# Order of the matmul pieces in the attention loop of a two-layer convolutional attention kernel: two scores side by side, later mixing

## The chip, the core and the metric

The kernel runs on one core of one Trainium2 chip. A core has five engines that run beside each other and wait for one another by semaphores: PE (TensorE, matrix products, with a weight load of its own that the profile calls PEld), DVE (VectorE), ACT (ScalarE), POOL (GpSimd) and SP (SyncE, which here only issues DMAs). The metric is the device time of one execution, in microseconds (us); lower is better.

## The reference, cut to what matters

Two attention layers run one after the other on x (8 images, 512 channels, 32 x 32 = 1024 tokens). The change touches the second layer alone. With 8 heads of 64 channels it computes, for every image b:

```python
q, k, v = (einsum('oc,bct->bot', w, xf).reshape(b, heads, hd, t) for w in (w_q, w_k, w_v))
attn = einsum('bhdq,bhdT->bhqT', q, k) * scale
attn = einsum('gh,bhqT->bgqT', w_head, attn)      # mixes the eight heads
attn = softmax(attn, axis=-1)
attn = (attn - mean) / sqrt(var + EPS)            # over all of a head's q and T
attn = attn * in_gamma + in_beta
out  = einsum('bhqT,bhdT->bhqd', attn, v)         # then w_proj, bias, residual
```

Each softmax needs the mixed scores of all heads, so the scores have to be regrouped between the two products: the first product gives one head at a time, the second wants the eight heads of a query beside each other on the partitions.

## The kernel before, in words

Everything here is in the class Attention1 (line 1616) and the loop over images at line 1901. For an image the 1024 queries are cut into NT = 8 blocks p of 128 queries. The work on a block has five stations:

- **scores(p, i)**, lines 1624 to 1643, i = 0 to 7: PE multiplies q and k for two heads and half of the keys (i = 0 to 3 are the first half, kh = 0; i = 4 to 7 the second, kh = 1) into a PSUM tile "m" of two banks. ACT copies it into an SBUF tile "raw" (L1643); for p = 0, DVE copies the odd ones (L1641). There are two raw buffers, so kh = 0 always has the one and kh = 1 the other.
- **regroup(kh, s)**, lines 1645 to 1650: SP issues two DMAs of 256 KB that read raw with a stride of partitions and write the tile "re", of which there is one. The four s are four sets of queries. A pair (kh, s) can start when the four copies of its half are done, and when the mixing of the block before has read its part of re.
- **mix(p, s)**, lines 1658 to 1682: PE multiplies re with the mixing weights into two PSUM tiles "m", each of which ACT turns into exponentials (L1676) in the tile "e" (two buffers). The call returns a function that issues the second of the two exponentials, so a caller can put other work between.
- **flip and moments**, lines 1684 to 1704: DVE transposes e into "et" (L1691) and takes statistics of e (L1702, four instructions). Once a block is complete, sums(p) (L1744 to L1748) turns them into "zz", and totals(p) (PE, L1755) multiplies zz; the reciprocals follow on DVE.
- **values(p, u, parts)**, lines 1706 to 1724: PE multiplies et and v (L1718) into the PSUM tile "a"; u is a half of the query sets, and the four parts of a half are a quarter each. leave(p, u), lines 1726 to 1737, copies the result out on ACT (L1734).

The PSUM tiles "m" come from a pool with three buffers (line 1273). Scores and mixings take them in turn, in the order in which they are called, so a piece waits until the tile three calls back has been copied or exponentiated. The engines take their instructions strictly in the order in which the program lists them.

**step(p, t, ag)**, line 1845, writes out that order by hand. For each p it is called with t = 0 to 3, and it works on three blocks at a time: the scores of block p, the mixing, flip and moments of block p - 1, and the rest of the values of block p - 2. For 2 <= p <= 7 PE's order is, with S for a score, M for a mixing, V for a part of the values, VV for two parts and z for the totals:

- t = 0: S0 S1 S2, VV (half 0 of block p - 2), M0
- t = 1: V (half 1, part 0), z, S3, M1
- t = 2: S4, V (half 1, part 1), S5, M2, VV (half 1, parts 2 and 3)
- t = 3: S6, M3, V (half 0 of block p - 1, part 0), S7, V (part 1)

M3's second exponentials are issued after S7's copy. DMAs go to SP's queue at the end of t = 1 (regroup of (0,0) and (0,1)), t = 2 ((0,2)) and t = 3 ((0,3), (1,0), (1,1), (1,2), (1,3)). At the end of t = 0, four or five further loads for the next image are queued there ("pieces", 128 KB each, L1304 and L1339). The agenda `ag` adds other work at fixed slots; its half-number slots hold entries only for p = 8.

In every image p = 0 has scores alone, p = 1 has no values of a block p - 2, and p = 8 has no scores; there, products for the next image (L1383) stand between the mixings.

Of the kernel before, what the change touches and what calls it, by code (L numbers as in the profile page):

```python
# [467 lines left out]
def tile_two_attention_layers(  # L468
# [19 lines left out]
    nc = tc.nc  # L488
# [205 lines left out]
    with ExitStack() as l0:  # L694
# [505 lines left out]
        for b in range(B):  # L1200
            more = b + 1 < B
            ag = Agenda()
# [61 lines left out]
    with ExitStack() as l1:  # L1264
# [180 lines left out]
        def k_leave():  # L1445
            for fn in due:
                fn()
            due.clear()
# [167 lines left out]
        class Attention1:  # L1616
# [228 lines left out]
            def step(self, p, t, ag):  # L1845

                new, old, older = p < NT, p >= 1, p >= 2
                if new and t != 1:
                    self.scores(p, 2 * t)
                    if t == 0:  # L1850
                        self.scores(p, 1)
                        self.scores(p, 2)
                if t == 3 and old:
                    second = self.mix(p - 1, 3)
                if t == 0 and older:
                    self.values(p - 2, 0, 2, 3)
                    self.leave(p - 2, 0)
                    self.sums(p - 2)
                    if p % 2 == 0 and p >= 4:
                        self.divide(p // 2 - 2, nc.gpsimd)  # L1860
                if t in (1, 2) and older:
                    self.values(p - 2, 1, t - 1)
                    if t == 1:
                        self.flip(p - 1, 0)
                        self.totals(p - 2)
                        self.moments(p - 1, 0)
                if t == 3 and old:
                    self.values(p - 1, 0, 0)
                if new and t:
                    self.scores(p, 2 * t + 1)  # L1870
                if t == 3 and old:
                    second()
                    self.values(p - 1, 0, 1)
                if t < 3 and old:
                    self.mix(p - 1, t)()
                ag.run(4 * p + t - 0.5)
                if t == 2 and older:
                    self.values(p - 2, 1, 2, 3)
                    self.leave(p - 2, 1)
                k_leave()  # L1880
                if p == 1 or old and t:
                    self.flip(p - 1, t)
                    self.moments(p - 1, t)
                if new:
                    for kh, s in (
                        (), ((0, 0), (0, 1)), ((0, 2),), ((0, 3), (1, 0), (1, 1), (1, 2), (1, 3)),
                    )[t]:
                        self.regroup(kh, s)
                if old and t == 0:
                    self.piece(4 if p < 5 else 5)  # L1890
                ag.run(4 * p + t)
# [9 lines left out]
        for b in range(B):  # L1901
            more = b + 1 < B
            a = Attention1(b)
            ag = Agenda()
# [142 lines left out]
```

## Time and profile before

| quantity | value |
|---|---|
| time, median of 3 runs (lowest, highest) | 4043.96 us (4040.07, 4045.96) |
| time of the profiled execution | 4037.07 us |
| its span, from the first to the last instruction | 4035.0 us |
| mean granted TensorE clock | 0.994 |
| PE busy | 3929.8 us (97%) |
| DVE busy | 2836.2 us (70%) |
| ACT busy | 1976.2 us (49%) |
| POOL busy | 129.1 us (3%) |
| regroup DMAs (re<-raw) | 1024 issues of 256 KB |
| scores of the second layer (L1631) | 523.8 us busy |
| mixings (L1665) | 352.8 us busy, idle before them 36.8 us |
| values (L1718) | 556.2 us busy |
| exponentials (L1676) | 502.9 us busy, 1023 ns each |
| copies into raw (L1643) | 471.3 us busy, 1017 ns each |
| flips (L1691) | 587.3 us busy, 2294 ns each |
| moments (L1702) | 633.8 us busy, 674 ns each |

The page gives each engine's busy time and its share of the span. A busy PE is not a PE without stalls: ends of matmuls are modelled, and a matmul that is held up in the middle of a group of sixteen counts as busy. What a piece costs is therefore read from the timeline, as the distance from its first matmul to the first matmul of the next piece. The second layer begins at about 1800 us of the span. One "round" below is the stretch from one z of the timeline to the next.

### The profile page before, as it was taken

The numbers are of one execution on the slowest core, as the hardware profiler recorded it, in microseconds if no ns is written. First come the engines' busy times: TensorE is split into PE (matmuls) and PEld (weight loads), VectorE is DVE, ScalarE is ACT, GpSimd is POOL, SyncE is SP. The second block draws the span as 40 slices with busy tenths as digits, with TensorE's granted clock in tenths as the row PEclk, the third lists the DMA queues.
The fourth block names the chain that finished last, engine by engine and source line by source line (L and its number), as shares of the span: only waits on it lengthen the run. The fifth ranks groups of instructions, "written<-read, shape, count | busy, mean of one in ns | idle before, by whom it ended". The sixth has DMA issues, their size and how long they took to land. (4 is left out here: it accounts for less than half of the span.)

```text
span 4035.0 us, 95990 instructions
## 1 busy us (share of the span) xinstructions
PE 3929.8 (97%) x41932; PEld 1825.9 (45%) x41932; DVE 2836.2 (70%) x4124; ACT 1976.2 (49%) x2431; POOL 129.1 (3%) x150
## 2 busy tenths in 40 slices
PE   8999999999999999999999999999999999999997
PEld 4353535343443435344544544544544444445354
DVE  4748475756667575847949859769769679588597
ACT  1727263544535362616617437347257166175274
POOL 0000000000000000000000001000000000000010
PEclk9999999999999999999999999999999999999998
DMA  3313131211111211227738739559469287396384
GB/s 126 113 47 116 45 119 48 87 41 58 72 66 51 82 56 61 77 80 201 195 116 222 194 105 233 157 144 232 131 168 226 93 213 201 106 224 187 112 216 127
DMA packets 268636, 519.12 MB, mean 129 GB/s; under 512 B 49840, under 2 KB 84912, under 8 KB 261552
## 3 DMA queue, kind: packets, MB, share of 16 engines
q1 hardware_dynamic: 261664, 497.96, 43.1%
q0 software_dynamic: 6544, 14.94, 1.5%
q8 instruction: 331, 5.42, 0.6%
q14 instruction: 97, 0.79, 0.1%
HBM read 197.16 MB, written 46.92 MB: 60 GB/s over the span
## 5 line engine op out<-in xcount | busy, mean ns | idle before, releaser
L1691 DVE STREAM_TRANSPOSE et<-e 128x2048 f32<-128x2048 f32 x256 | 587.3, 2294 | 115.7 <-ACT e L1676 110.2
L1718 PEld LDWEIGHTS a<-et,v 128*64 128x64 f32 x16384 | 508.4, 138 | 287.7 <-issue 228.3
L1702 DVE BATCH_NORM_STATS2 bn<-e 128x6 f32<-128x512 f32 x1024 | 633.8, 674 | 0.0
L1086 ACT ACTIVATE e<-s 128x1024 f32<-128x1024 f32 x512 | 497.2, 1026 | 234.5 <-PE s L1081 234.0
L1643 ACT COPY raw<-s 128x1024 f32<-128x1024 f32 x480 | 471.3, 1017 | 276.6 <-PE s L1631 243.7
L1676 ACT ACTIVATE e<-m 128x1024 f32<-128x1024 f32 x512 | 502.9, 1023 | 148.6 <-PE m L1665 63.1
L1718 PE MATMUL a<-et,v 128*64 128x64 f32 x16384 | 556.2, 225 | 5.7 <-DVE et L1691 5.3
L1094 DVE TENSOR_TENSOR zacc<-zacc,e 128x1024 f32<-128x1024 f32 x384 | 468.7, 1221 | 89.9 <-ACT e L1086 68.0
L1631 PE MATMUL s<-k,q 64*64 64x512 f32 x4096 | 523.8, 608 | 8.0 <-DVE q L1497 3.1
L1081 PE MATMUL s<-q,k 64*64 64x512 f32 x4096 | 490.1, 593 | 2.3 <-ACT e L1086 2.3
L1107 PE MATMUL a<-e,v 64*64 64x512 f32 x4096 | 484.1, 589 | 0.0
L1665 PE MATMUL m<-re,wmix 32*32 32x512 f32 x8192 | 352.8, 606 | 36.8 <-DMA re<-raw 30.7
L1107 PEld LDWEIGHTS a<-e,v 64*64 64x64 f32 x4096 | 156.7, 133 | 282.8 <-issue 282.5
L1081 PEld LDWEIGHTS s<-q,k 64*64 64x64 f32 x4096 | 147.9, 133 | 275.2 <-issue 241.0
L1458 PE MATMUL pv<-wv,y 128*128 128x512 f32 x480 | 213.8, 601 | 0.0
L1631 PEld LDWEIGHTS s<-k,q 64*64 64x64 f32 x4096 | 121.7, 131 | 201.6 <-issue 81.4
L1665 PEld LDWEIGHTS m<-re,wmix 32*32 32x32 f32 x8192 | 73.4, 103 | 232.9 <-ACT e L1676 68.0
L1734 ACT COPY q<-a 64x256 f32<-64x256 f32 x256 | 93.8, 366 | 139.8 <-PE a L1718 137.4
L1770 POOL DMA_DIRECT2D zd<-rz x56 | 34.6, 619 | 3466.4 <-DMA y<-x 1854.0
L1458 PEld LDWEIGHTS pv<-wv,y 128*128 128x128 f32 x480 | 89.9, 191 | 118.0 <-issue 111.3
L1462 ACT COPY v<-pv 128x512 f32<-128x512 f32 x30 | 17.6, 585 | 220.4 <-PE pv L1458 220.4
L1092 DVE TENSOR_TENSOR zacc<-e,e 128x1024 f32<-128x1024 f32 x64 | 78.3, 1223 | 56.1 <-ACT e L1086 56.1
(315 smaller groups left out, 3946.8 us busy)
## 6 DMA issues: line engine op xcount, KB each, us to landing
re<-raw SPq DMA_DIRECT2D x1024, 256.0 KB
left_q<-left_q SPq DMA_DIRECT2D x17, 1792.0 KB
left_p<-left_p SPq DMA_DIRECT2D x17, 1792.0 KB
left_k<-left_k SPq DMA_DIRECT2D x10, 1792.0 KB
x<-in_x_dram SPq DMA_DIRECT2D x32, 512.0 KB
rzb<-zd SPq DMA_DIRECT2D x128, 128.0 KB
x<-x SPq DMA_DIRECT2D x64, 256.0 KB
left_v<-left_v SPq DMA_DIRECT2D x8, 1792.0 KB
```

The costliest lines, as they stand in the source:

```text
L1081: nc.tensor.matmul(ps[c * D : c * D + D, m], k[r, hp, k0 : k0 + D], q[r, hp, ts(f, FB)], start=True, stop=True,)
L1086: nc.scalar.activation(e[i], ps, AF.Exp, scale=S0 * S0)
L1094: nc.vector.tensor_add(zacc[g], zacc[g], e[i])
L1107: nc.tensor.matmul(acc[g][a][m * D : m * D + D], v[rows, kc, ts(2 * hp + m, D)], e[i][rows, m], start=(kc == 0), stop=(kc == NG - 1),)
L1458: nc.tensor.matmul(ps[:, m], y_t[b][:, c, ts(2 * i + m, P)], w[:, c], start=(c == 0), stop=(c == NCC - 1),)
L1631: nc.tensor.matmul(ps[c * D : c * D + D, m], qo_t[b][r, p, hp, ts(c, D)], k_t[b][r, hp, ts(kh, FB)], start=True, stop=True,)
L1643: nc.scalar.copy(dst, ps)
L1665: nc.tensor.matmul(ps[a // 2][c * 32 : c * 32 + 32, a % 2].rearrange("p (r kb k) -> p r kb k", r=2, k=32), wmix[rows].rearrange("p g i -> ...
L1676: nc.scalar.activation(e[:, :, 2 * h : 2 * h + 2].rearrange("p r a k -> p a r k"), ps[h].rearrange("p a (r k) -> p a r k", r=2), AF.Exp,)
L1691: nc.vector.transpose(self.et[p, u].rearrange("p kb (r st a) g q -> p st kb r (a g q)", r=2, st=2)[:, st], self.e[p, s].rearrange("p r a ( ...
L1702: nc.vector.bn_stats(self.bn[p][:, s, a], e[:, :, a].rearrange("p r k -> p k r"))
L1718: nc.tensor.matmul(acc[two * D : two * D + D, s].rearrange("p (x q) -> p x q", q=4), v_t[b][:, kb, ts(g, D)], et[:, kb, :, g], start=(kb = ...
```

## The change

Only the body of step changes; the same pieces are issued, and each the same number of times. For t = 0 and t = 1 the order stays. For 2 <= p <= 7 the order of t = 2 and t = 3 on PE becomes:

- t = 2: V (half 1, part 1), S4, S5, VV (half 1, parts 2 and 3), M2
- t = 3: S6, V (half 0, part 0), M3, S7, V (part 1)

On ACT, leave(p - 2, 1) now stands ahead of M2's exponentials; S4's and S5's copies stay ahead of both. M3's first exponentials still stand ahead of S7's copy and the second ones behind it. DVE's order and SP's order stay as they are: flip 2, moments 2 and the regroup of (0,2) are listed after M2 in both. For p = 1, which has no values of a block p - 2, only t = 3 changes. For p = 0 and p = 8 nothing changes.

```diff
@@ -1845,38 +1845,58 @@
             def step(self, p, t, ag):
 
                 new, old, older = p < NT, p >= 1, p >= 2
-                if new and t != 1:
-                    self.scores(p, 2 * t)
-                    if t == 0:
-                        self.scores(p, 1)
-                        self.scores(p, 2)
-                if t == 3 and old:
-                    second = self.mix(p - 1, 3)
-                if t == 0 and older:
-                    self.values(p - 2, 0, 2, 3)
-                    self.leave(p - 2, 0)
-                    self.sums(p - 2)
-                    if p % 2 == 0 and p >= 4:
-                        self.divide(p // 2 - 2, nc.gpsimd)
-                if t in (1, 2) and older:
-                    self.values(p - 2, 1, t - 1)
-                    if t == 1:
+                if t == 0:
+                    if new:
+                        for i in range(3):
+                            self.scores(p, i)
+                    if older:
+                        self.values(p - 2, 0, 2, 3)
+                        self.leave(p - 2, 0)
+                        self.sums(p - 2)
+                        if p % 2 == 0 and p >= 4:
+                            self.divide(p // 2 - 2, nc.gpsimd)
+                    if old:
+                        self.mix(p - 1, 0)()
+                    ag.run(4 * p - 0.5)
+                elif t == 1:
+                    if older:
+                        self.values(p - 2, 1, 0)
                         self.flip(p - 1, 0)
                         self.totals(p - 2)
                         self.moments(p - 1, 0)
-                if t == 3 and old:
-                    self.values(p - 1, 0, 0)
-                if new and t:
-                    self.scores(p, 2 * t + 1)
-                if t == 3 and old:
-                    second()
-                    self.values(p - 1, 0, 1)
-                if t < 3 and old:
-                    self.mix(p - 1, t)()
-                ag.run(4 * p + t - 0.5)
-                if t == 2 and older:
-                    self.values(p - 2, 1, 2, 3)
-                    self.leave(p - 2, 1)
+                    if new:
+                        self.scores(p, 3)
+                    if old:
+                        self.mix(p - 1, 1)()
+                    ag.run(4 * p + 0.5)
+                elif t == 2:
+                    if older:
+                        self.values(p - 2, 1, 1)
+                    if new:
+                        self.scores(p, 4)
+                        self.scores(p, 5)
+                    if old and not new:
+                        self.mix(p - 1, 2)()
+                    ag.run(4 * p + 1.5)
+                    if older:
+                        self.values(p - 2, 1, 2, 3)
+                        self.leave(p - 2, 1)
+                    if old and new:
+                        self.mix(p - 1, 2)()
+                else:
+                    if new:
+                        self.scores(p, 6)
+                        if old:
+                            self.values(p - 1, 0, 0)
+                            second = self.mix(p - 1, 3)
+                        self.scores(p, 7)
+                        if old:
+                            second()
+                            self.values(p - 1, 0, 1)
+                    else:
+                        self.mix(p - 1, 3)()
+                        self.values(p - 1, 0, 0, 1)
+                    ag.run(4 * p + 2.5)
                 k_leave()
                 if p == 1 or old and t:
                     self.flip(p - 1, t)
```

## The prediction

> **What bounds the kernel now.** I read the page first, then the table of busy time by stretches of time, then PE's timeline round by round, then the waits of the mixing's line. The page gives PE 97%, which says little here, so I looked at the part that the change touches. A round runs from one z (L1755) to the next; 40 rounds (t = 1 of p = 2 to t = 1 of p = 7, eight images) hold only S, M, V and z. The table takes the five rounds of each image as one stretch; the columns are length, busy time by engine, granted clock, DMA share and rate.
>
> ```profile
> core 0: us, PE busy (x) PEld busy (x) DVE busy (x) ACT busy (x) POOL busy (x), PEclk, DMA share, GB/s
> 2139.90:2251.30 111.40, 107.34 (x2260) 55.65 (x2260) 101.68 (x141) 87.06 (x103) 10.52 (x12) 1.00 0.91 229
> ...
> sum 880.90, PE 861.03 PEld 447.27 DVE 816.61 ACT 688.21 POOL 84.88; mean PE 107.63 PEld 55.91 DVE 102.08 ACT 86.03 POOL 10.61
> ```
>
> A round takes 880.9 / 40 = 22.0 us. DVE is busy for 102.1 / 5 = 20.4 of that and the DMA engines 0.91 of it: three resources are close together. PE's own floor I take from the timeline, piece by piece, as the least distance from a piece's first matmul to the next one's: z 0.30, S3 1.02, M1 1.20, S4 1.02, V 1.08, S5 1.02, M2 1.09, VV 2.02, S6 1.02, M3 1.09, V 1.08, S7 1.02, V 1.08, S0 to S2 2.73, VV 2.02, M0 1.07, V 0.98: 20.8 us. The mean round is 1.2 us above it, in three places: M2 (mean 1.66, so 0.57 over), the VV ahead of M0 (2.29, 0.27 over) and the V ahead of z (1.22, 0.24 over); 0.1 is elsewhere. Two neighbouring rounds show all three.
>
> ```profile
> 2166.19 1.09 PE L1631 MATMUL s<-k,q 64*64 64x512 f32 x8
> 2167.16 1.93 ACT L1643 COPY raw<-s 128x1024 f32<-128x1024 f32 x2 [0.98 <-DMA re<-raw]
> 2167.21 2.15 PE L1665 MATMUL m<-re,wmix 32*32 32x512 f32 x32
> 2169.29 2.08 PE L1718 MATMUL a<-et,v 128*64 128x64 f32 x64
> ...
> 2182.79 1.15 PE L1665 MATMUL m<-re,wmix 32*32 32x512 f32 x32 [1.37 <-DMA re<-raw]
> ```
>
> The first row is S5, the third M2, and ACT's row between them is the copies of S4 and S5. S4 was multiplied by 2165.1, but ACT stood idle for 0.98 us until a regroup landed: S4's copy overwrites the raw buffer of kh = 1, which the last regroup (1,3) of the block before still reads. M2's second tile takes the PSUM buffer of S4 (three calls back), so M2 lasts 2.08 instead of 1.09. The last row is M0, which waits for (1,0). The next round has neither, and pays at z, for DVE's statistics:
>
> ```profile
> 2190.49 1.16 PE L1665 MATMUL m<-re,wmix 32*32 32x512 f32 x32
> 2190.63 1.01 ACT L1643 COPY raw<-s 128x1024 f32<-128x1024 f32 x1 [0.27 <-PE s L1631]
> 2191.58 2.09 PE L1718 MATMUL a<-et,v 128*64 128x64 f32 x64
> ...
> 2206.09 0.21 DVE L1748 TENSOR_TENSOR zz<-zz,bn 128x32 f32<-128x32 f32 x1
> ...
> 2206.45 0.39 PE L1755 MATMUL z<-sel,zz 128*64 128x32 f32 x4 [0.60 <-DVE zz L1748]
> ```
>
> In 39 of the 40 rounds M2's length follows the start of S4's copy: 4.5 us after z gives 1.09, 5.1 gives 1.54 to 1.58, 5.6 gives about 2.1. In the 24 rounds with a stall that follow another of the 40, the copy starts 11.8 to 13.1 us, middle 12.4, after the end of S7's copy in the round before; and S7's copy ends 9.5 us after S4's starts (5.66 to 15.16). That is a loop of 12.4 + 9.5 = 21.9 us, next to the mean round of 22.0: **the round is set by the loop S4's copy, S5's copy, M2, VV, S6, M3, V, S7, S7's copy, four regroups.** The waits ahead of the mixings' matmuls show copies and regroups among their releasers:
>
> ```profile
> its engine sat idle before it (us, times) until:
>   ACT e L1676: 71.3, 95
>   issue: 66.0, 69
>   ACT raw L1643: 49.8, 72
>   ACT q L1734: 46.5, 53
>   DMA re<-raw: 30.7, 18
> ```
>
> **The change, part by part.** Nothing is added or removed, and SP, POOL and DVE keep their order, so every row above keeps its duration and only the starts move. With the same rows the new round runs, in us after z: S3 0.3, M1 1.3, V 2.4, S4 3.5, S5 4.4, VV 5.4, M2 7.4, S6 8.5, V 9.55, M3 10.6, S7 11.7, V 12.7, S0 13.8, VV 16.6, M0 18.6, V 19.65, next z 20.6.
>
> *M2 behind VV.* M2 comes at 7.4 instead of 5.6. ACT's work behind S4's copy is S5's copy, leave and then M2's exponentials: 1.02 + 1.02 + 0.74 = 2.8 us. M2's matmuls end at 8.5 and the exponentials start 0.14 later, so S4's copy may start as late as 8.67 - 2.8 = 5.9 at no cost. It comes at 13.9 (end of S7's copy) + 12.4 - 21.5 (the round that I forecast) = 4.8. So the 0.57 goes. The loop through ACT becomes 2.8 + 1.94 (exponentials) + 1.0 (S6's copy) + 1.0 (M3's first exponential) + 1.0 (S7's copy) = 7.8, plus 12.4: 20.2, below PE's floor.
>
> *S4 next to S5.* A score by itself costs 1.02, three in a row 2.73, so 0.91 each. One change of shape less: 0.11. The S4 of before also waited for S3's copy (M1 lasts 1.20 there, other mixings 1.07 to 1.09): another 0.11, which V now covers. But M2 and M3 now each have a score behind them. If that itself is what costs 1.20, I lose 0.22; the floor is 20.6 to 20.9. The Trainium skill's "TensorEngine Tiling (Array Packing)", section Key Properties, says that changing the tiling mode drains the engine; it gives no time; by it t = 2 and t = 3 have ten drains where there were eleven.
>
> *V ahead of M3.* V needs the flips 0 and 1; the second ends at 6.8 + 2.3 = 9.1 after z, V starts at 9.55: 0.45 to spare. M3 needs M2's second exponential (8.67 + 1.94 = 10.6): level. S7 needs S6's copy (10.6 + 1.0 = 11.65): level. S1 needs M3's second exponential (11.86 + 1.0 + 1.0 + 1.0 = 14.9, asked for at 14.7): up to 0.2 lost.
>
> *What is late next.* DVE. From M0's start to flip 0 are 3.3 us (2182.79 to 2186.09), from there to the end of sums 20.2 (to 2206.30), 0.15 to z, and 18.6 from z to the M0 after next: 42.3 us for two rounds, 21.1 each. On top of it, M0's regroup: the natural distance from S7's copy to M0 is 4.7 us, and in half of the rounds it took longer, up to 6.5; 0.27 in the mean. And S0's copy: it waits for (0,3), which leaves at M3's end and took 4.5 to 6.35 us, middle 5.1: 11.7 + 5.1 = 16.8; three copies and leave later (2.84 + 0.74) M0's exponentials start at 20.4, 0.4 later than M0 allows. Some of these overlap; I add 0.4, so a round is **21.5**.
>
> Sum: 40 x (22.0 - 21.5) = 20 us. The round from p = 7 to p = 8, eight times, has the same M2 (mean 1.78, 0.69 over); I take 0.5 each, 4 us. For p = 1, M3 behind V: the old M3 there lasts 1.99, waiting for M2's exponential, so V could fill 1.1 us; but M3's exponential then waits for DVE's moments as before (1.10 us before 2129.91), and S1 for M3. Between +1.1 and -1.1 I take zero (9 us either way over eight images). With rounding **25 us less**: 4037 - 25 = 4012 for the profiled execution (span 4035, 2 us around it). The median of 4044 lies 7 above that execution: **4019**.
>
> *A rule that speaks against it.* In the round into p = 8 no score stands between the values and M0, and PE idles up to 3.5 us for (1,0). After an idle time of 2.63 us the granted clock fell to a half:
>
> ```profile
> 1988.00:1990.00 2.00, 2.00 (x14) 0.87 (x4) 1.77 (x4) 1.76 (x2) 0.00 (x0) 0.50 1.06 247
> ```
>
> After 2.61 us in another image it stayed at 1.00. S7's copy keeps its distance to M0 here, and (0,3) leaves about 1.1 us nearer to (1,0), so this wait may grow by 0 to 0.3. The Trainium skill's "TensorE: Matmul & The Clock Gate", Part 1, puts the idle window at about 3.4 us and the clock at a half behind it; by that rule the longest waits alone are at risk, and the sum stays. By the row, the two of the seven rounds whose products (L1383) still last 3.63 us could go the way of the others (4.25 to 5.31): 3 us more, 4022.
>
> **The rivals.** *The gain is given back* (4032 to 4048). DVE is 20.4 of 22.0 busy, DMA 0.91; rounds without an M2 stall were not all short (20.9 to 22.7, among them M0 waits of 1.8 us). If the regroups' landing sets the pace, the 0.57 reappears ahead of M0 and z: about 4042. For it: 2706.0, where M2 took 1.09 and the round 22.68. Against: in the two rounds shown, cut into half microseconds, the DMA share falls below 0.4 ahead of (0,3) and of (1,0), so there is room. This is also the case in which the change does not do what it says.
>
> *Slower* (4048 to 4068). (0,2) leaves at 8.5 instead of 7.3 to 7.8, (0,3) at 11.7, (1,0) at 13.9, so three transfers stand closer. M0 needs S1's copy, 1.95 us after S0's start. At 6.35 us for (0,3), S0's copy starts at 18.1, M0 at 20.0, the exponentials 0.35 later still: a round of 22.4, 40 x 0.4 = 16 us more, 4060. It decides from about 6.0 us on (19.65 for M0, a round of 22.0); 5.1 is the middle now.
>
> **How the numbers follow.** Forecast (a round of 21.1 to 21.8, 4004 to 4032): 0.62. Better still: 0.04. Given back: 0.21. Slower: 0.13. The range 4004 to 4048 holds the first and the third, 0.83; the forecast's own is 4004 to 4032. About 0.2% (8 us) is what a measurement of this kernel can tell from no change: below 4036 lie the first two and 0.05 of the third, 0.71; within, 0.16 of the third and 0.02 of the last, 0.18; above, 0.11.
>
> **What would show it.** Right: M2 at 1.1 to 1.2 us in every round, S4's copy still waiting in places without a longer M2, more idle time at z for L1748, 40 rounds of about 21.5. Wrong: M0 waiting over 0.6 us in the mean; flips 2 or 3 waiting for exponentials; V ahead of M3 waiting for flip 1; S0's copy over 17.7 after z.

## The result, and the profile after

After the change the kernel takes 4059.03 us (median of 8 runs, 4048.92 to 4068.75); the kernel before takes 4040.66 us on the same chip (8 runs, 4033.92 to 4049.93). The ratio is 1.0044, 95% interval 1.0029 to 1.0059: slower by 18 us, where 4019 was forecast. The profiled execution took 4054.86 us, its span is 4052.6 us (before 4035.0), the clock 0.993. Where no interval is given, numbers below are from the one profiled execution of a kernel.

The first view is again the table of busy time, with the five rounds of an image as one stretch (the row is the same image as before):

```profile
core 0: us, PE busy (x) PEld busy (x) DVE busy (x) ACT busy (x) POOL busy (x), PEclk, DMA share, GB/s
...
2143.54:2255.61 112.07, 105.32 (x2267) 57.11 (x2263) 101.64 (x141) 85.84 (x103) 10.53 (x12) 1.00 0.90 228
...
sum 891.67, PE 841.38 PEld 456.75 DVE 812.43 ACT 680.05 POOL 84.35; mean PE 105.17 PEld 57.09 DVE 101.55 ACT 85.01 POOL 10.54
```

A round takes 891.67 / 40 = 22.29 us instead of 22.02: 40 x 0.27 = 10.8 us. PE is busy for 19.7 us less, so PE now stands still for longer. The round from p = 7 into p = 8 takes 0.78 us more in the mean (27.25 against 26.47, seven images), 7.0 us with the last image. The two together are 17.8, and the spans differ by 17.6. In PE's timeline a round looks like this (start, time, idle time ahead and what ended it):

```profile
1901.94 0.37 PE L1755 MATMUL z<-sel,zz 128*64 128x32 f32 x4
...
1905.48 1.95 PE L1631 MATMUL s<-k,q 64*64 64x512 f32 x16
1907.36 2.09 PE L1718 MATMUL a<-et,v 128*64 128x64 f32 x64
1909.38 1.14 PE L1665 MATMUL m<-re,wmix 32*32 32x512 f32 x32
...
1912.57 1.29 PE L1665 MATMUL m<-re,wmix 32*32 32x512 f32 x32
1913.78 1.09 PE L1631 MATMUL s<-k,q 64*64 64x512 f32 x8
...
1915.88 2.81 PE L1631 MATMUL s<-k,q 64*64 64x512 f32 x24
1918.62 2.08 PE L1718 MATMUL a<-et,v 128*64 128x64 f32 x64
1922.10 1.25 PE L1665 MATMUL m<-re,wmix 32*32 32x512 f32 x32 [1.39 <-DMA re<-raw]
...
1924.26 0.37 PE L1755 MATMUL z<-sel,zz 128*64 128x32 f32 x4
```

S4 and S5 are one row of sixteen matmuls, and M2 behind VV (1909.38) runs without a stall. Then M0 stands still until a regroup lands, and starts at 1922.10. From VV to M0 are 3.48 us, where VV itself takes 2.02. In the prediction's measure, from the start of a piece to the start of the next (mean of 40 rounds, in us):

```
before: z 0.31  S3 1.04  M1 1.23  S4 1.02  V 1.08  S5 1.02    M2 1.66  VV 2.02
after:  z 0.31  S3 1.03  M1 1.15  V 1.14   S4 and S5 1.88     VV 2.02  M2 1.07
before: S6 1.02  M3 1.09  V 1.09   S7 1.02  V 1.10  S0-S2 2.74  VV 2.29  M0 1.09  V 1.22   sum 22.02
after:  S6 1.03  V 1.08   M3 1.23  S7 1.02  V 1.08  S0-S2 2.74  VV 3.19  M0 1.17  V 1.15   sum 22.29
```

M2 is 0.59 shorter, and S4 and S5 are 0.16 shorter; the VV ahead of M0, up to M0's start, is 0.90 longer. The waits ahead of the mixings say the same: the regroup rises from 30.7 us in 18 waits to 70.9 in 45, and the waits for leave (L1734) fall from 46.5 to 8.5.

```profile
its engine sat idle before it (us, times) until:
  DMA re<-raw: 70.9, 45
...
  ACT q L1734: 8.5, 5
```

**Which transfer is late, and by how much.** In the trace each of these DMAs raises its semaphore sixteen times; I read that as once for each of the 16 DMA engines. The last of (1,0)'s increments ends M0's wait: after the change M0 starts 0.09 to 0.14 us behind it in the 48 cases there are from p = 2 to p = 7 (six for each image). Means of the 48, in us ("apart": from the issue of (0,3) to that of (1,0); "15 of 16" and "last": from the issue of the second DMA of (1,0)):

```
                 apart   15 of 16   last    end of S7's copy to M0
before           3.02    3.83       4.11    4.93   (least 4.68)
after            1.99    4.12       5.00    5.79   (least 4.65)
```

Three things stand in this table. (1,0) is issued 1.0 us nearer to (0,3), because M3, whose end lets (0,3) go, now stands directly ahead of S7, whose copy lets (1,0) go. The fifteenth engine is done 0.29 us later. And the last engine is now 0.88 us behind the fifteenth, instead of 0.28. So of the 0.89 us that (1,0) loses, a third is shared by the engines and two thirds are the last one's. The DMA share by half microseconds shows the difference; before, in the round at 2184.4, (0,3) was issued at 2195.96 and (1,0) at 2198.98 and 2199.55:

```profile
core 0: us, PE busy (x) PEld busy (x) DVE busy (x) ACT busy (x) POOL busy (x), PEclk, DMA share, GB/s
...
2198.50:2199.00 0.50, 0.50 (x20) 0.43 (x20) 0.50 (x2) 0.50 (x2) 0.00 (x0) 1.00 1.04 287
2199.00:2199.50 0.50, 0.50 (x8) 0.22 (x12) 0.50 (x2) 0.50 (x1) 0.00 (x0) 1.00 0.80 201
2199.50:2200.00 0.50, 0.50 (x12) 0.17 (x7) 0.50 (x2) 0.38 (x1) 0.00 (x0) 1.00 0.10 33
2200.00:2200.50 0.50, 0.50 (x8) 0.15 (x4) 0.50 (x2) 0.00 (x0) 0.00 (x0) 1.00 0.60 152
2200.50:2201.00 0.50, 0.50 (x8) 0.15 (x4) 0.50 (x2) 0.28 (x1) 0.00 (x0) 1.00 0.96 188
```

(0,3)'s packets run dry at 2199.5, and an engine that was behind has caught up: fifteen engines of (0,3) were done at 2199.96 and the last at 2200.62, but of (1,0) at 2203.31 and 2203.33. After the change, in the round shown above, (0,3) was issued at 1914.03 and (1,0) at 1915.98 and 1916.55:

```profile
core 0: us, PE busy (x) PEld busy (x) DVE busy (x) ACT busy (x) POOL busy (x), PEclk, DMA share, GB/s
...
1915.50:1916.00 0.50, 0.50 (x20) 0.43 (x20) 0.50 (x2) 0.50 (x2) 0.00 (x0) 1.00 1.04 234
1916.00:1916.50 0.50, 0.50 (x8) 0.22 (x12) 0.50 (x2) 0.50 (x1) 0.00 (x0) 1.00 1.04 250
1916.50:1917.00 0.50, 0.50 (x12) 0.17 (x7) 0.50 (x2) 0.38 (x1) 0.00 (x0) 1.00 1.06 266
1917.00:1917.50 0.50, 0.50 (x8) 0.15 (x4) 0.50 (x2) 0.00 (x0) 0.00 (x0) 1.00 1.07 283
1917.50:1918.00 0.50, 0.50 (x8) 0.15 (x4) 0.50 (x2) 0.00 (x0) 0.00 (x0) 1.00 1.00 254
```

There is no pause. Fifteen engines of (0,3) were done at 1918.96, the last at 1920.08; and of (1,0) at 1920.94 and 1921.96. The lag of 1.1 us goes on into (1,0), and M0 starts at 1922.10.

**Theory (merge):** the move of M3 next to S7 takes the pause between (0,3) and (1,0), so what (0,3) still has queued on the slowest engine delays (1,0), and M0 waits for it. **Rivals:** the later (0,2), which leaves with M2 (8.9 us after z instead of 7.6), is what crowds the transfers; or the DMAs' bytes, or VectorE, set the pace of a round at about 22 whatever PE's order is; or PE's order alone sets when M0 can start.

### The profile page after: what moved, and what is told of

It reads as the page before. It is cut to its first block, busy times and chain, and to the rows that moved or that the text cites. A ratio compares the mean times of both kernels' runs of the same rounds, so it can differ in the third digit from the quotient of the medians.

```text
span 4052.6 us, 95942 instructions
## 1 busy us (share of the span) xinstructions
PE 3904.0 (96%) x41932; PEld 1837.8 (45%) x41932; DVE 2832.9 (70%) x4124; ACT 1964.8 (48%) x2431; POOL 128.5 (3%) x150
## 5 line engine op out<-in xcount | busy, mean ns | idle before, releaser
L1631 PE MATMUL s<-k,q 64*64 64x512 f32 x4096 | 514.9, 607 | 6.3 <-DVE q L1497 3.1
L1665 PE MATMUL m<-re,wmix 32*32 32x512 f32 x8192 | 331.9, 608 | 80.9 <-DMA re<-raw 70.9
L1734 ACT COPY q<-a 64x256 f32<-64x256 f32 x256 | 94.1, 368 | 165.0 <-PE a L1718 163.0
L1462 ACT COPY v<-pv 128x512 f32<-128x512 f32 x30 | 17.6, 586 | 218.6 <-PE pv L1458 218.6
```

The source lines that it names most:

```text
L1631: nc.tensor.matmul(ps[c * D : c * D + D, m], qo_t[b][r, p, hp, ts(c, D)], k_t[b][r, hp, ts(kh, FB)], start=True, stop=True,)
L1665: nc.tensor.matmul(ps[a // 2][c * 32 : c * 32 + 32, a % 2].rearrange("p (r kb k) -> p r kb k", r=2, k=32), wmix[rows].rearrange("p g i -> ...
```

## The experiments

Diffs are against the changed kernel, where nothing else is said; ratios are to the kernel before, run beside them on the same chip. "Round" and "wait" are means of 40 rounds, a wait being what lies above the least distance seen.

**Half of the change each: the new t = 2 alone, and the new t = 3 alone.**

```diff
 e1: t = 3 as before
                         if old:
-                            self.values(p - 1, 0, 0)
                             second = self.mix(p - 1, 3)
+                            self.values(p - 1, 0, 0)
 e2: t = 2 as before
-    V, S4, S5, VV, M2
+    S4, V, S5, M2, VV
```

> This kernel has the change's order in t = 2 (V, S4, S5, VV, M2) and the old order in t = 3 (S6, M3, V, S7, V). Theory (the merge): the second layer lost its time where M3 moved next to S7, because the regroup (0,3), which leaves at M3's end, then runs into (1,0), which leaves after S7's copy; the 16 DMA engines have no pause between the two any more, so an engine that has fallen behind (one that fetched 16 KB of instructions) is still behind at (1,0), for which M0 waits. Here M3 and S7 are apart again: second half of (1,0) about 4.2 us from issue to landing as before (5.05 in the changed kernel), M0's stretch VV back to about 2.3 to 2.5. But V no longer covers M2's second exponential, so M3 should last about 1.1 longer: a round of 21.9 to 22.3, time 4035 to 4050. Rival (the late (0,2)): it is M2's move that pushes (0,2), and with it everything behind it in the DMA queue; then (1,0) still takes about 5 us, VV stays at 3.2 and M3's 1.1 comes on top: a round near 23.2, time about 4090.

> This kernel has the old order in t = 2 (S4, V, S5, M2, VV) and the change's order in t = 3 (S6, V, M3, S7, V). Theory (the merge): (0,3) and (1,0) leave about 1.9 us apart instead of 3.0, so (1,0) lands late (about 5 us from issue) and VV ahead of M0 lasts about 3.2; S4's copy still waits for (1,3) and M2 still lasts about 1.6: a round of 22.4 to 22.9, time 4050 to 4075. Rival (the late (0,2)): (0,2) leaves as before, so (1,0) takes 4.1 to 4.3, VV 2.3; a round of 21.7 to 22.0, time 4030 to 4042.

Measured: e1 4051.29 us, 1.0038 (1.0024 to 1.0051); e2 4056.09 us, 1.0050 (1.0036 to 1.0063). With M3 back behind S6, the two transfers are 3.03 us apart again, the last increment of (1,0) comes after 4.12, and VV to M0 takes 2.27, as before the change: the wait is gone although (0,2) still leaves late. With the old t = 2 and V ahead of M3 they are 1.96 apart, it comes after 4.59, and M0 waits 0.67. So the wait belongs to t = 3, and the rival of the late (0,2) falls as a cause by itself. It has a share, though: the shorter distance alone costs (1,0) 0.48 us (4.59 against 4.11), the late (0,2) alone nothing (4.12), and both together 0.89 (5.00). For e2 I had expected about 5 us and a wait of about 1.2 (3.2 for VV), so the forecast of the merge by the distance alone was too high. But e1 is slower than the kernel before as well: M3 then pays. Its row in PE's timeline of e1:

```profile
2171.18 1.10 PE L1631 MATMUL s<-k,q 64*64 64x512 f32 x8
2172.53 2.06 PE L1665 MATMUL m<-re,wmix 32*32 32x512 f32 x32 [0.25 <-ACT e L1676]
```

M3 waits for M2's exponentials, starts 0.32 later, and lasts 1.99 in the mean instead of 1.09 (0.90 more). Neither half is good by itself: M2 behind VV needs the V ahead of M3, and the V ahead of M3 brings (0,3) and (1,0) together.

**The merge by itself: PE's order as changed, half of (0,3) left out; and, as a control, half of (0,2).**

```diff
-            def regroup(self, kh, s):
+            def regroup(self, p, kh, s):
-                for r in range(2):
+                for r in range(1 if p and (kh, s) == (0, 3) else 2):    # e12: (0, 2)
...
-                        self.regroup(kh, s)
+                        self.regroup(p, kh, s)
```

From p = 1 on these two kernels leave out half of a regroup, so a mixing reads half of its operand from p = 0: their times show what the transfer costs and are no times of the whole computation.

> The changed kernel, every instruction of TensorE in its place, with one of the two DMAs of regroup (0,3) left out from p=1 on (M3 then reads half of its operand from p=0: part of the computation is left out). Merge theory (a backlog of (0,3) on one of the 16 engines is carried on into (1,0), which is issued 2.0 us behind it): the second half of (1,0) lands 4.0 to 4.2 us after its issue instead of 5.0, the 0.90 us that M0 waits beyond the kernel before falls to 0 to 0.2, and rounds fall from 22.29 to 21.4 to 21.9 (less than 0.9 where another wait follows, as in the kernel with both covers): 4059 - 16 to 43 = 4016 to 4043 us. Rival (TensorE's order alone sets when M0 can start, the distance of the two transfers has no part in it): t of (1,0) 4.8 to 5.0, M0's wait as it is, 4055 to 4062 us.

> The control: the changed kernel with one of the two DMAs of regroup (0,2) left out from p=1 on instead (part of the computation is left out), as many bytes fewer in a round, but not in the transfer directly ahead of (1,0). Merge theory: (0,3) may be through 0.3 to 0.6 us sooner, (1,0) still 4.6 to 5.0 after its issue, M0 waits at least 0.5 us longer than in the kernel before, 4045 to 4059 us. If instead the bytes of the whole round (or the number of DMAs) set the pace, this kernel gains as much as the one with half of (0,3).

Measured: e11 4019.92 us, 0.9954 (0.9941 to 0.9968); e12 4043.57 us, 1.0010 (1.0001 to 1.0019). In e11 the last increment of (1,0) comes after 4.11, the engine that is last lags by 0.30, and VV to M0 takes 2.30: within 0.02 the numbers of the kernel before (4.11, 0.28, 2.29), at a distance of 1.96 and with every PE instruction where the change has put it. The rival of PE's order alone falls. In e12, with as many bytes fewer, it comes after 4.61 and VV to M0 still takes 2.81. It gains about 0.4 of what e11 gains, more than I had expected (4045 at least), since with (0,2) shorter, (0,3) is through 0.56 sooner (4.05 instead of 4.61). The rival of the bytes or VectorE falls with the pair: with the same bytes in a round as e12, and VectorE as busy as before (816 us in the 40 rounds), e11's round is 0.39 us shorter (21.57 against 21.96). I read (0,2), (0,3) and (1,0) as one queue. The last row of e11's table of busy time, with five rounds of every image as one stretch:

```profile
sum 862.63, PE 836.99 PEld 453.64 DVE 816.38 ACT 680.00 POOL 84.44; mean PE 104.62 PEld 56.71 DVE 102.05 ACT 85.00 POOL 10.55
```

862.63 / 40 = 21.57 us a round; the prediction had said 21.5. And what is late next is z, for DVE's statistics, as the prediction had it: in e11 z waits for zz (L1748) in 22 places, after the change in 7. Of the list of what ended the idle time ahead of z in e11 (us, times):

```profile
  DVE zz L1748: 20.1, 22
```

**The distance restored by a later S7** (t = 3: S6, V, M3, V, S7).

```diff
                             second = self.mix(p - 1, 3)
+                            self.values(p - 1, 0, 1)
                         self.scores(p, 7)
...
-                            self.values(p - 1, 0, 1)
```

> The changed kernel with S7 moved behind the second V: t = 3 is S6, V, M3, V, S7. (0,3) and (1,0) are then 3.0 us apart again, but one V less stands between S7 and M0. Theory (the merge): the second half of (1,0) takes about 4.2 us from its issue instead of 5.05, its last engine lags by about 0.4 instead of 0.9; M0 comes 0.65 + 4.2 + 0.13 = 5.0 after the end of S7's copy instead of 5.86, so although S7 is 1.1 us later M0 is only 0.2 to 0.3 later than in the changed kernel: a round of 22.3 to 22.7, time 4055 to 4080. Rival (the landing takes 5.05 after its issue whatever stands ahead of it): M0 is 1.1 us later: a round near 23.3, time about 4100.

Measured: 4056.55 us, 1.0052 (1.0038 to 1.0066), round 22.23. The transfers are 3.03 apart and (1,0)'s last increment comes after 4.02: the lateness is gone. The time is not, since S7's copy comes a V (1.08) later and PE's way from there to M0 is shorter by the same. M0 now waits in every round for the transfer's ordinary duration (0.44 us at least). The rival, 5.05 whatever stands ahead, falls.

**A cover for M0: a V between VV and M0, taken from between M0 and M1 (e5); both covers, with the other V moved up too (e7); the old t = 2 and t = 3 with both covers (e10).**

```diff
 e5 (e7 keeps z behind its V)              e7 beside it
 t = 0: S0 S1 S2, VV, +V, M0               t = 0: S0 S1 S2, VV, +V, M0
 t = 1: -V, S3, z, M1                      t = 1: S3, V (part 1), z, M1
 t = 2: V, S4, S5, VV, M2                  t = 2: S4, S5, VV, M2
 e10: as e7, with t = 2: S4, S5, M2, VV and t = 3: S6, M3, V, S7, V
```

> The changed kernel with one part of the values (half 1, part 0) moved from behind M0 to ahead of it, and z behind S3, so that M0 keeps its place before z in the round but has 1.08 us more of PE work between S7 and itself. Theory: (1,0)'s landing is what ends PE's wait ahead of M0 (1.17 us in the mean over the least distance), and what the change gained in M2 is really there: the wait falls to 0.2 to 0.4, a round of 21.2 to 21.7 (DVE's two-round loop sets 21.1), and the round into p = 8 loses another 1 us each: time 4000 to 4030, faster than before. Rival (DVE or the DMA engines' rate sets the round, and M0's wait is only where it shows): the round stays at 22.0 to 22.3, the wait moves to z or to S0's copy; time 4040 to 4060.

> The changed order with the values matmul of half 1, part 0 put between VV and M0, and that of part 1 in its old place between M0 and M1 (t0: S0-S2, VV, V, M0; t1: S3, V, z, M1; t2: S4, S5, VV, M2; t3: S6, V, M3, S7, V). The p=8 round is as in the changed kernel. Merge theory (the round is long because M0 stands idle for the regroup (1,0), which lands about 1 us late behind (0,3)): V fills 0.9 of the 0.90 us that M0 waited beyond before, and M1 keeps a V of 0.9 ahead of it, so the stall of 0.85 that the kernel with a cover for M0 alone showed in M1 (1.94) doesn't come. Round 22.3 - 0.8 to 1.1 = 21.2 to 21.5, M1 at most 1.2, time 4059 - 41 x 0.8 to 1.1 = 4012 to 4026 us, faster than before. Rival (the DMAs or VectorE set the pace of a round, at about 22): another wait grows by what M0 gains, round 22.0 to 22.2, 4036 to 4045 us.

> The kernel before's order in t2 and t3 with both covers (V ahead of M0, V between M0 and M1; t2: S4, S5, M2, VV; t3: S6, M3, V, S7, V). If the change's move of M2 behind VV is worth its 0.57 us once M0 is covered, this round is 0.6 to 1.5 longer than that of the kernel with both covers and the new t2, since M2 now follows S5 with no V in between and waits for M1's exponentials: 22.0 to 22.6, 4035 to 4060 us. Rival (something else sets the pace at 22): as long as the kernel with both covers, within 5 us.

Measured: e5 4041.93 us, 1.0015 (1.0006 to 1.0024); e7 4040.33 us, 1.0002 (0.9993 to 1.0010); e10 4042.56 us, 1.0010 (1.0001 to 1.0018); rounds 22.14, 21.91, 22.12. In e5 the V also stands ahead of M0 in the round into p = 8; in e7 and e10 that round has no cover. All three take back most of the loss, and both e5 and e7 missed what I had expected of them (rounds of 21.2 to 21.7 and 21.2 to 21.5). In e5, M1 pays (1.94): no V stands between M0 and M1 any more to hide M0's exponentials. In its timeline the last row is M1:

```profile
2161.66 1.14 PE L1665 MATMUL m<-re,wmix 32*32 32x512 f32 x32
2162.73 1.11 PE L1631 MATMUL s<-k,q 64*64 64x512 f32 x8
2163.76 0.42 PE L1755 MATMUL z<-sel,zz 128*64 128x32 f32 x4
2164.26 2.05 PE L1665 MATMUL m<-re,wmix 32*32 32x512 f32 x32
```

In e7, M1 is at 1.15, as forecast, and M0 still waits 0.68 beyond a VV and a V without a wait (2.95); but S4 and S5, with no V behind M1 any more, take 2.34 instead of 1.88, and the V ahead of M3 comes 0.23 later. The timeline of e7 shows both new waits:

```profile
2255.66 1.09 PE L1631 MATMUL s<-k,q 64*64 64x512 f32 x8 [0.23 <-ACT e L1676]
...
2261.12 1.15 PE L1718 MATMUL a<-et,v 128*64 128x64 f32 x32 [0.25 <-DVE et L1691]
```

A V covers one wait at a time, and there are more waits than Vs. In e10 M2 takes 2.21 (1.07 in e7): the move of M2 is worth 1.1 there, and 0.6 of it goes back at M0 (3.63 in e7, 3.00 in e10), with M3 next to S7 in e7. The two kernels lie 2 us apart, and their intervals overlap. So the rival of a pace of about 22 is not shown wrong by these three kernels; e11 beside e12 shows it wrong.

**The round into p = 8** (e8: the kernel before with only its p = 8 reordered, the products L1383 of between M0 and M1 ahead of M0, the last values of half 1 ahead of z; e9: the same on e7). The diff shows e8's edit in the wording of the new step; t = 2 and t = 3 are those of before.

```diff
+                    if not new:
+                        ag.run(4 * p - 0.5)
                     if old:
                         self.mix(p - 1, 0)()
                     ag.run(4 * p - 0.5)
...
+                        if not new:
+                            self.values(p - 2, 1, 1, 2, 3)
+                            self.leave(p - 2, 1)
                         self.totals(p - 2)
...
-                    if older:
+                    if older and new:
                         self.values(p - 2, 1, 1)
...
-                    if older:
+                    if older and new:
                         self.values(p - 2, 1, 2, 3)
                         self.leave(p - 2, 1)
```

> The kernel before with the p=8 round alone reordered: the products that stood between M0 and M1 (3.6 us) stand ahead of M0, and the values of half 1, parts 1 to 3, stand ahead of z. The wait of M0 in the p=8 round (2.6 to 3.5 us in the kernel before, 2.65 to 4.75 after the change) is then filled. If that wait is idle TensorE time on the path that sets the end, 7 rounds gain some 2.6 to 3.5 us less what M1 loses without the products ahead of it (0 to 1 us): 4036 - 12 to 24 = 4012 to 4024 us. Rival (the two halves' exponentials set the p=8 round's length whatever stands between): no change, 4032 to 4042 us.

> The order of the kernel with both covers (V ahead of M0 and V ahead of M1, fifth and sixth score in a row) with the reordered p=8 round. If the two waits are independent, the gains add: 22.3 - 0.8 to 1.1 in 40 rounds and 1.6 to 3.5 in 7: 4059 - 32 to 44 - 11 to 24 = 3991 to 4016 us, faster than both kernels. By the rival of each: 4032 to 4045 us.

Measured: e8 4011.86 us, 0.9933 (0.9921 to 0.9945); e9 4005.89 us, 0.9922 (0.9909 to 0.9935), both faster than the two kernels of the study. M0's wait there, in PE's timeline after the change, in the image with the longest one:

```profile
3405.96 3.02 PE L1718 MATMUL a<-et,v 128*64 128x64 f32 x96
3413.73 2.02 PE L1665 MATMUL m<-re,wmix 32*32 32x512 f32 x32 [4.75 <-DMA re<-raw]
```

The same place in e9's timeline (the view begins inside the first row, which has eight products in all):

```profile
3372.76 2.74 PE L1383 MATMUL pk<-y,left_k 128*128 128x512 f32 x6
3375.78 1.15 PE L1665 MATMUL m<-re,wmix 32*32 32x512 f32 x32 [0.28 <-DMA re<-raw]
3376.86 3.95 PE L1718 MATMUL a<-et,v 128*64 128x64 f32 x128
```

The products fill 3.6 us of it, and M0 lasts 1.15 instead of 2.02, as the clock is not down. z stands behind S3 and a V in e7 and e9, so rounds at the end of an image are not compared with theirs; from the start of an image's last score to its last z are 42.3 us before, 43.8 after the change, 44.9 in e7, 39.0 in e8 and 39.5 in e9 (means of seven): in e8, 7 x 3.3 = 23 us of the 27 that the ratio says. e9 lies in the range that I had given (3991 to 4016), but by luck: its 40 rounds are no shorter than e7's (21.90 and 21.91, not 21.2 to 21.5), and the end of an image gains 4.3 us on the changed kernel instead of 1.6 to 3.5.

## Why the prediction was wrong, point by point

- **M2's stall goes: right.** M2 takes 1.07 in every round; 0.59 gone, 0.57 forecast. S4's copy starts 4.94 after z, 4.8 forecast.
- **S4 next to S5, and what the mixings lose: right in size.** The pair takes 1.88, where two single scores took 2.04: 0.16 gained for the 0.11 forecast. M1 falls from 1.23 to 1.15. M3 takes 1.23, as feared, but not for the score behind it, since it takes 1.22 in e3 too, with a V behind. M2's second exponential ends 0.1 after M3's start, by ACT's row of 1910.72 (1.94 long, so 1912.66) and PE's of 1912.57: I read this as M3's other tile waiting for it; I had called that level.
- **V ahead of M3, S1: right.** No wait for flip 1; S0 to S2 take 2.74.
- **p = 1 at zero: right.** From the first score of an image to its first z are 47.98 us, before 47.84 (seven images): 1 us in all.
- **What is late next: here the step failed.** "... the natural distance from S7's copy to M0 is 4.7 us, and in half of the rounds it took longer, up to 6.5; 0.27 in the mean." I took 0.27 over into the new round. It measured 1.17, and "M0 waiting over 0.6 us in the mean" was the first sign that I had named for being wrong. What I read as a mean wait was a wait with next to no reserve: before, M0 started 0.09 or 0.14 us behind (1,0)'s landing in 23 of the 48 cases, which is the value of a mixing that waits, and 0.18 to 0.36 behind it in the other 25. So (1,0) had less than 0.3 us to spare, and what it loses beyond that is lost by M0. I had also worked out that (0,3) leaves "about 1.1 us nearer to (1,0)" (measured 1.03), and had used it for the round into p = 8 alone, at 0 to 0.3. It holds in every round and costs 0.9. e11 takes this one term away and has a round of 21.57, where I had said 21.5: the other terms of the round add up to what I forecast. That its time, 4020, lies next to the 4019 of the forecast is partly luck: it gains 18.4 us on the kernel before beside it, where I had forecast 25, and 4019 was reckoned from 4044, a median of three runs that eight runs put at 4041.
- **DVE as the next limit: right, but seen only where (1,0) is less late.** z waits for zz 22 times in e11 and 15 times in e12; in the changed kernel, with 7, M0 hides it.
- **The round into p = 8: wrong sign.** I took 4 us off; it costs 0.78 more each. Beyond the 2.95 us that three V take, M0 comes 2.90 to 4.82 us later there, 3.70 in the mean of seven, before 2.91. But PE is earlier at this point, so M0 starts only 0.10 us later after z than before (19.72 and 19.62). The other 0.68 lies behind M0's start, where 3.82 us up to the next z are at half clock instead of 2.41 (means of seven). In e11, M0 starts at 18.80, 0.82 earlier than before, and the round is no shorter (26.55): 4.24 us are at half clock. That is the risk of the rule that I had named against the forecast and had left out of the sum; that the clock makes all of the difference is not shown by itself.
- **The rival "slower" (4060) had the time, in part by luck, and half of the mechanism.** It named the three transfers that come closer, but let them act through S0's copy, which waits for (0,3). That copy does start later, 17.72 after z, where over 17.7 was named as the sign; yet M0 starts 0.36 to 3.01 us behind the end of that copy and 0.09 to 0.14 behind (1,0)'s landing.
- **The rival "the gain is given back" (4042) had the place.** It said that the 0.57 reappears ahead of M0 if the regroups' landing sets the pace; it was 0.90. The evidence that I set against it, "there is room" in the DMA share, was the very pause that the change closes: I read it from the old order and did not ask whether the new one keeps it.

Not settled: which engine lags and why (below). That 16 KB fetches are the cause is a coincidence in time, seen in the three kernels for which it is given below; no run took the fetches away.

## What to carry to other kernels

Before a mean wait is carried over into a new order, look at its distribution: a consumer that starts within a few tenths of its transfer's landing in every round has next to no reserve, and whatever delays the transfer is paid in full. When a change moves the instruction that releases one transfer towards the one that releases the next, work out the new distance between the two issues against the time that the first takes; idle time between transfers is what lets a late one catch up, and it counts as used. An instruction that hides a wait in one place hid another where it came from: name that one before you move it.

## What the runs showed of the hardware

- **The last of sixteen increments falls behind, and in these traces that goes with instruction fetches.** The changed kernel's page lists queue q8 (packets, MB, share of 16 engines), in the line below: 16 KB a packet, and a packet takes 1.13 us in the median. Where such a packet is under way between the first issue of (1,0) and its landing, the last increment lags the fifteenth by 1.13 us in the mean (36 rounds after the change), elsewhere by 0.10 (12 rounds); before by 0.48 (27) and 0.02 (21), in e11 by 0.37 (38) and 0.04 (10). A late landing makes that stretch longer, so this split favours the link: in a fixed stretch of 3.8 us from the second issue on, it is 1.19 (28) and 0.44 (20) after the change.

```profile
q8 instruction: 331, 5.42, 0.6%
```

- **The granted clock falls on a grid, so the length of a wait does not say by itself whether M0 meets the half clock.** In e11 M0 took 2.26 us after 2.56 us of idle PE in the round into p = 8, and 1.08, at the full clock, after 3.20 in another image. The Trainium skill's "TensorE: Matmul & The Clock Gate", Part 1, gives an idle window of about 3.4 us; of the waits here, one below it met the half clock and another did not. The traces say why: from 1830 us to the last z, the twelve kernels have 94 stretches at half clock, each 3.41 or 6.83 us long, and within a trace all start a whole number of steps of 3.413 us apart. Of the steps of this grid, all 88 in which PE idled for 2.03 us or more were followed by the half clock; of the 7365 at full clock with less than 1.83 us, one was. So the step has the length of the window that the page gives, but it need not be idle as a whole. In e11's second case the clock fell at 1984.10, when M0, from 1982.62 on, had run. In the wait of 4.75 us shown above, the granted clock (the number ahead of the DMA share) fell about 2 us after PE had stopped at 3408.98, by the table of busy time of the changed kernel:

```profile
3410.00:3411.00 1.00, 0.00 (x0) 0.00 (x0) 1.00 (x1) 0.00 (x0) 0.68 (x1) 1.00 1.03 291
3411.00:3412.00 1.00, 0.00 (x0) 0.00 (x0) 1.00 (x3) 0.00 (x0) 0.00 (x0) 0.50 1.05 248
```

- **A score in a row is cheaper than a score alone by 0.16 us**: 1.02, 1.88 and 2.74 us for one, two and three. Four in a row, S7, S0, S1 and S2 in e3, take 4.17, more than 4 x 1.02; I read that as the wait for the tile three calls back. The Trainium skill's "TensorEngine Tiling (Array Packing)", Key Properties, has the drain at a change of mode without a time; these differences bound it here, but no run shows that the drain is what they hold.
